# Linear attention: the pieces of FP4 unpacking moved away from the first q G products, and the sums for these products put in another order

## The chip, the cores and the metric

The kernel runs on one core of a Trainium2 chip. The core has five engines with an instruction queue each: TensorE (PE in the profile, its loading of weights PEld), VectorE (DVE), ScalarE (ACT), GpSimd (POOL) and SyncE (SP, here only an issuer of DMAs). Each engine takes its own instructions in their order, and waits on semaphores for the others. The metric is the device time of one execution in microseconds; the median of several runs counts.

## The reference, cut to what matters

Four blocks follow each other: a linear attention with a layer norm, an FP4 feed-forward part, a gated linear attention, and a routed feed-forward part. The change lies in the first one, on an input of 2 batches with 1024 rows of 512 values in float32:

```
q = elu(x Wq^T) + 1;   k = elu(x Wk^T) + 1;   v = x Wv^T        # 16 heads of 32
kv = k^T v  (per head);   z = 1 / (q . sum of k + 1e-6)
out = q kv z;   x = layernorm(x + out Wo^T)
```

The feed-forward part that comes next has weights in FP4, eight values in an int32, with a float16 scale per 128 inputs. Their unpacking (codes to float32) belongs to that part, but is done while the attention runs.

## The kernel before

**Blocks and batches.** The 2048 rows are 4 blocks of 512, two per batch; `b` counts batches, `i = 2b` and `j = 2b + 1` are a batch's blocks. The main loop is at L629 to L669: for each batch the k products of its blocks, then the q products, and in between the pieces of other work.

**Products by seven.** A 512x512 by 512x512 product is done with seven half-size products in place of eight (`by_seven`, L338). It needs sums of quarters: `sums_of_weights` (L330; T1, T2, T4, T3 from the weight's quarters B11 to B22, each one DVE instruction at L335) and three sums of x (S1 at L356, S2 at L357, S3 at L358, and again S2 at L373). The products accumulate into a bank of PSUM, `grow`: after each of them the partial sum is copied out by ACT (c11 at L363, c21 at L370, c22 at L376) or read by elu at L304 and L306, before PE adds the next product to the same bank. A second bank (`P` in the profile) takes the two products that are not part of the chain; DVE adds it at L366, L377 and L384. `elu1` (L299) is ACT, ACT, DVE: L304, L305, L306.

**k^T x and G.** `add_xk` (L393) accumulates k^T x of a batch in four banks; DVE and ACT copy it into G (L408). `values` (L452) multiplies by Wv (`vk`, copied by ACT at L463), `G_rows` (L465) by Wo (`gp`, 32 small matmuls at L473, copied into G by ACT at L477). G is now the batch's kv and Wo in one 512x512 matrix, so that out Wo^T is q G. `G_rows` then computes the four sums of G in the room `TG`: in batch 0 the tile staged[2], in batch 1 the slot in which Wo stood. The room's fourth quarter serves for S1 of q.

**q.** `weigh` (L436) divides each row of q by its sum with k: per 128 rows L441, L443, L444, L445 and L447, all on DVE. `turned` (L486) transposes 128 rows of q on PE (`qTp`, L217) and ACT copies them into qT (L492). `o_products` (L494) is q G by seven for a block: S1 (L515), S2 (L516), the difference A11 - A21 (L517), then seven products (L507), each followed by an add to x on DVE (L513). As elsewhere PE adds to `grow` only when the add to x has read it. It is a generator: `some_o(blk, n)` runs it n products on. For block 3 the product q G is a plain one, `whole_o` (L547).

**The 27 pieces of unpacking.** `unpack` (L244) is: a DMA issued by SP that brings 16 rows of packed words, each repeated on 8 partitions, into the tile `pk` (L248); two DVE instructions on it (L251, a pair of shifts, and L252, a mask); and a copy by ACT from float16 to float32r with a factor (L254). The pool has two `pk` buffers. The first 16 pieces are of 704 columns (352 KB, into wgu), the last 11 of 512 (256 KB, into wdn). `job(n)` (L616) puts n pieces at a point of the main loop.

**What sets the order.** A scheduler with a cost model of its own chooses each engine's order of instructions from the program's order and from what depends on what. `behind()` keeps PE's order to the program's, and `issue_after(anchor)` keeps a piece behind the last elu that was written before it. On the chip each engine then follows that order strictly: an instruction that waits for a DMA stops everything behind it on its engine.

**The steps of the loop.** `run(products, *others)` runs a generator of products and after each `yield` the next list of other steps. In batch 0 the q products of block 1 carry `turns(0, ...)`, `G_rows` and the q G products of block 0; in batch 1 the k products of block 2 carry the q G products of block 1; the q products of block 3 carry `G_rows` and the q G products of block 2, and `split_some`, which prepares the next part's input (L231, L232). Just behind the loop stand the scales of the next part: one small transpose `pg` (L679), a copy, and five small DVE instructions (L280, L281, L683, L684, L685); the first users are L807 (ACT) and L809 (DVE).

Of the kernel before, what the change touches and what calls it, by code (L numbers as in the profile page):

```python
# [10 lines left out]
F32 = mybir.dt.float32  # L11
# [10 lines left out]
P = 128  # L22
# [51 lines left out]
def body(ctx: ExitStack, tc: tile.TileContext, a: dict, out: bass.AP):  # L74
    nc = tc.nc
# [20 lines left out]
    def acc_bank(name):  # L96
        return bank("acc", name)
# [5 lines left out]
    staged = [  # L103
        wfp4.tile([P, to - at, C], F32, tag=f"wdn{i}", name=f"staged{i}")
        for i, (at, to) in enumerate(zip(wdn_parts, wdn_parts[1:]))
    ]
# [20 lines left out]
    def place_w(i, name):  # L127
        return wpool.tile([P, KC, C], F32, tag=f"A{i}", name=name)
# [27 lines left out]
    t, src = new_xT(0)  # L156
# [84 lines left out]
    wk = s1.enter_context(tc.tile_pool(name="s1", bufs=2))  # L241
# [85 lines left out]

    pieces_of = lambda t: t.rearrange("p (k c) -> p k c", k=2)

    def sums_of_weights(w, rooms):  # L330

        B11, B12, B21, B22 = (w[:, 2 * e : 2 * e + 2, 256 * o : 256 * o + 256] for e in range(2) for o in range(2))
        T1, T2, T4, T3 = (*rooms, B12)[:4]
        for dst, x, y in ((T1, B12, B11), (T2, B22, T1), (T4, B21, T2), (T3, B22, B12)):
            nc.vector.tensor_sub(dst, x, y)  # L335
        return T1, T2, T3, T4

    def by_seven(x, w, T, rooms, pairs, ready):  # L338
# [3 lines left out]
        T1, T2, T3, T4 = T  # L342
        S1, S2, S3 = rooms

# [11 lines left out]
        nc.vector.tensor_add(S1, A21, A22)  # L356
        nc.vector.tensor_sub(S2, S1, A11)  # L357
        nc.vector.tensor_sub(S3, A11, A21)  # L358
# [9 lines left out]
        yield  # L368
        product(grow, S2, T2, False)
        nc.scalar.copy(c21, p)  # L370
        side = mm_bank("P7")
        p7 = product(side, S3, T3, True)
        nc.vector.tensor_sub(S2, A12, S2)  # L373
        yield
# [4 lines left out]
        yield  # L379
        product(grow, S2, B22, False)  # L380
        elu1(c12, p)
# [8 lines left out]
    pairs_of, mv_of, G_of, acc_of, ksum_of = {}, {}, {}, {}, {}  # L390
# [59 lines left out]
    vkm_of, qT, TG, o_of, parts = {}, {}, {}, {}, []  # L450

    def values(b):  # L452
# [9 lines left out]

        nc.scalar.copy(vkm_of[b], vk.rearrange("p (c d) -> p c d", c=KC))  # L463

    def G_rows(b):  # L465


        gp = [acc_bank("gp") for _ in range(4)]
        quad = lambda i: slice(32 * i, 32 * i + 32)
        for j in range(4):  # L470
            for c in range(KC):
                with behind():
                    last_pe[0] = nc.tensor.matmul(  # L473
                        gp[j][quad(c)], vkm_of[b][quad(j), c, quad(j)], Wo[quad(j), c], start=True, stop=True
                    ).ins
        for c in range(KC):
            nc.scalar.copy(G_of[b][:, c], gp[c])  # L477

        room = staged[2] if b == 0 else place_w(3, "TG")
        rooms = slices(room, 0, 3)  # L480
        if b:

            rooms.append(pieces_of(wk.tile([P, 512], F32, tag="qT3", name="T3", bufs=1)))
        TG[b] = sums_of_weights(G_of[b], rooms), pieces_of(room[:, 3])

    def turned(blk, i):  # L486
        if i == 0:
# [6 lines left out]
    def o_products(blk):  # L494

        A11, A12, A21, A22 = (qT[blk][:, 2 * e : 2 * e + 2, 256 * t : 256 * t + 256] for t in range(2) for e in range(2))
        G = G_of[blk // 2]
        B11, _, B21, B22 = (G[:, 2 * e : 2 * e + 2, 256 * o : 256 * o + 256] for e in range(2) for o in range(2))
        (T1, T2, T3, T4), S1 = TG[blk // 2]
        S2 = pieces_of(wk.tile([P, 512], F32, tag="qS", name="qS", bufs=1))  # L500

        def product(ps, a, b, first, t, o):

            with behind():
                for r in range(2):
                    for k in range(2):
                        ins = nc.tensor.matmul(  # L507
                            ps[:, 256 * r : 256 * r + 256], a[:, k, r * P : (r + 1) * P], b[:, k],
                            start=first and r == 0 and k == 0, stop=k == 1, skip_group_check=True,
                        ).ins  # L510
            last_pe[0] = ins
            x = x_t[blk][:, 2 * t : 2 * t + 2, 256 * o : 256 * o + 256]
            nc.vector.tensor_add(x, x, ps.rearrange("p (r c) -> p r c", r=2))  # L513

        nc.vector.tensor_add(S1, A21, A22)  # L515
        nc.vector.tensor_sub(S2, S1, A11)  # L516
        nc.vector.tensor_sub(A21, A11, A21)  # L517
        grow = acc_bank("grow")
        product(grow, A11, B11, True, 0, 0)
        yield  # L520
        product(acc_bank("P2"), A12, B21, True, 0, 0)
        yield
        product(grow, S2, T2, False, 1, 0)
        nc.vector.tensor_sub(A12, A12, S2)
        yield
        side = acc_bank("P7")
        product(side, A21, T3, True, 1, 1)
        yield
        product(grow, S1, T1, False, 1, 1)
        yield  # L530
        product(side, A22, T4, False, 1, 0)
        yield
        product(grow, A12, B22, False, 0, 1)
        yield
        mv = mv_of[blk] = sp.tile([P, 4, 2], F32, tag="mv", name="mv")
        with tc.issue_after(weighed[0]):
            for i in range(4):
                row_stats(mv[:, i], x_t[blk][:, i])
            layernorm(x_t[blk], mv, by=nc.gpsimd)
        yield  # L540
# [57 lines left out]
    def some_xk(blk, *part):  # L598
        return [lambda i=i: add_xk(blk, i) for i in part]

    def turns(blk, *part):
        return [lambda i=i: turned(blk, i) for i in part]

    def some_o(blk, n):

        def one():
            if blk not in o_of:
                o_of[blk] = o_products(blk)
            next(o_of[blk])

        return [one] * n
# [4 lines left out]
    job = lambda n: [lambda: unpack_some(n)]  # L616
# [7 lines left out]
    step = lambda f, *x: [lambda: f(*x)]  # L624
# [4 lines left out]
    for b in range(B):  # L629
        i, j = 2 * b, 2 * b + 1  # L630
        if b:
            run(
                k_products(i),
                turns(1, 0, 1) + job(1), job(1),
                turns(1, 2, 3) + some_o(1, 1) + job(1), some_o(1, 2) + job(1), some_o(1, 5) + job(1),
            )
        q_ready = [] if b else step(q_weights)
        run(
            k_products(j), [],
            some_xk(i, 0, 1) + job(2), some_xk(i, 2) + job(1) + q_ready, some_xk(i, 3) + job(1), job(1 + b),  # L640
        )
        if b == 0:
            Ts["q"] = sums_of_weights(Wq, slices(staged[0], 0, 3))
        else:

            Tq = place_w(1, "Tq")
            for n in range(3):
                nc.scalar.copy(Tq[:, n], staged[0][:, n])
            Ts["q"] = (*slices(Tq, 0, 2), Ts["q"][2], *slices(Tq, 2, 3))
            S_rooms[0] = pieces_of(Tq[:, 3])  # L650
        run(
            q_products(i, lambda t: weigh(i, t)), [],
            some_xk(j, 0, 1) + job(1 + b), some_xk(j, 2) + step(spread_ksum, b) + job(1), some_xk(j, 3) + job(1 + b),
        )
        if b == 0:
            xT[2] = load_xT(2)
        split = [step(split_some, n) if b else [] for n in range(4)]
        rings["free"] = (rings["sum"][(turn_of["sum"] + 1) % 2],)
        run(
            q_products(j, lambda t: None),  # L660
            step(values, b),
            turns(i, 0, 1) + split[0] + job(1 - b),
            turns(i, 2, 3) + split[1] + step(G_rows, b),
            some_o(i, 2) + split[2] + some_o(i, 1) + job(1 - b),
            step(all_free) + some_o(i, 1) + step(weigh, j, 0) + split[3] + some_o(i, 3) + step(weigh, j, 1) + some_o(i, 1)
            + job(1 - b),
        )
        if b == 0:
            xT[3] = load_xT(3)  # L669
# [94 lines left out]
    with tc.tile_pool(name="s2", bufs=1) as wk2:  # L764
# [24 lines left out]
        class Chunk:  # L789
# [28 lines left out]
            def step(self, e, k, by):  # L818
                self.product(e, k)
                self.end(e, k, by)  # L820

        class Normed:
# [41 lines left out]
            def rest(self):  # L864

                for i in range(4):
                    x = x_t[self.blk][:, i]
                    nc.vector.scalar_tensor_tensor(x, self.y[:, i], self.ms[:, i : i + 1], x, ALU.mult, ALU.add)
                yield
                for i in range(4):  # L870
                    row_stats(self.mv[:, i], x_t[self.blk][:, i])
                layernorm(x_t[self.blk], self.mv)
# [179 lines left out]
    wk = s3.enter_context(tc.tile_pool(name="s3", bufs=1))  # L1052
# [368 lines left out]
    turns, last_hp = [0], [None]  # L1421
# [335 lines left out]
    wk = ctx.enter_context(tc.tile_pool(name="s4", bufs=2))  # L1757
# [4 lines left out]
    room = xT_tile("row")  # L1762
# [78 lines left out]
```

## Time and profile before

| | us |
|---|---|
| median of 3 runs | 934.13 |
| the 3 runs | 934.13, 934.41, 929.76 |
| the profiled execution | 929.62 |
| its span, first to last instruction | 927.8 |
| PE busy in the span | 900.6 (97%) |
| DVE busy | 685.2 (74%) |
| ACT busy | 377.3 (41%) |
| POOL busy | 257.4 (28%) |
| mean granted TensorE clock | 0.998 |

The prediction shows lines of four views. The page gives busy times and shares of the chain that ended last. A table by stretches has the length first, then the busy time of PE, PEld, DVE, ACT and POOL with the number of instructions, the granted clock, the DMA share and GB/s. A timeline has the start, the duration, the engine, the line of the code and the operation with its output and input tile; the bracket gives the idle time before it and what ended it. For a tile the profile lists its instructions and the time from a DMA's issue to its landing. Times in the text are from the span's start. The part of the program that the change touches runs from about 45 to 230 us.

### The profile page before, as it was taken

How to read it: one execution, taken by the hardware profiler on the slowest of the kernel's cores; microseconds unless marked ns; L12 is line 12 of the kernel's file. 1: busy time of each engine (PE TensorE's matmuls, PEld its weight loads, DVE VectorE, ACT ScalarE, POOL GpSimd, SP SyncE). 2: the span in 40 equal slices, each digit the busy share in tenths (PEclk: the TensorE clock that was granted, in tenths of full speed). 3: DMA queues.
4: the chain of work that ended last, by engine and by line, in shares of the span. 5: the costliest groups of instructions: out<-in, count | busy, mean ns of one | idle time of the engine just before them, and what ended most of it. 6: DMA issues, size and time to landing. Idle time of an engine off the chain costs nothing.

```text
span 927.8 us, 10966 instructions
## 1 busy us (share of the span) xinstructions
PE 900.6 (97%) x4037; PEld 698.6 (75%) x4037; DVE 685.2 (74%) x1310; ACT 377.3 (41%) x632; POOL 257.4 (28%) x229
## 2 busy tenths in 40 slices
PE   9999999999999999999998899999999999999996
PEld 6668876687677877877785577788676888888886
DVE  2579994689677786786686876676978886898635
ACT  2345334353476876876873524130311222120000
POOL 1020075100563555564563111010061030000012
PEclk9999999999999999999999999999999999999999
DMA  8622221100300001001001400000023211230011
GB/s 321 220 82 77 77 70 46 58 1 1 125 1 1 1 0 42 5 1 45 1 1 46 192 12 1 1 1 1 1 92 136 91 47 46 91 136 1 9 39 46
DMA packets 26136, 50.17 MB, mean 54 GB/s; under 512 B 4799, under 2 KB 5483, under 8 KB 25570
## 3 DMA queue, kind: packets, MB, share of 16 engines
q1 hardware_dynamic: 23441, 44.34, 14.0%
q0 software_dynamic: 1920, 4.22, 1.2%
q10 hardware_dynamic: 720, 0.92, 0.3%
q8 instruction: 32, 0.52, 0.2%
q14 instruction: 23, 0.18, 0.1%
HBM read 41.03 MB, written 10.54 MB: 56 GB/s over the span
## 4 chain that ended last, share of the span: by engine, by line
PE 76%; DVE 15%; ACT 3%; POOL 3%; issue 2%; DMA 1%; POOLq 0%; SPq 0%; ACTq 0%; DVEq 0%
PE yp L1525 10%; PE hp L1441 9%; PE gatep L783 8%; PE yp L783 8%; PE upp L783 8%; PE go L1196 6%; PE xk L400 6%; PE grow L349 4%; PE P L349 3%; PE ao L547 1%; PE ao L1314 1%; POOL x L884 1%; PE grow L1280 1%; PE kp L573 1%; DVE cmp L1365 1%
## 5 line engine op out<-in xcount | busy, mean ns | idle before, releaser
L841 DVE TENSOR_TENSOR yp<-yp,ratio 128x512 f32<-128x512 f32 x160 | 103.4, 694 | 13.1 <-PE yp L783 12.6
L201 POOL TENSOR_TENSOR rs<-rs,table 128x4 f32<-128x4 f32 (+1 forms) x20 | 18.2, 911 | 302.0 <-DVE rs L200 301.8
L807 ACT ACTIVATE gatep<-gatep,scale 128x512 f32<-128x512 f32 x132 | 85.3, 658 | 23.2 <-PE gatep L783 19.6
L783 PE MATMUL gatep<-x1Th,wgu 128*128 128x512 f32 x176 | 73.6, 418 | 0.6 <-ACT gatep L807 0.4
L783 PE MATMUL yp<-wdn,hlo 128*128 128x512 f32 x176 | 70.2, 399 | 3.4 <-POOL hlo L816 3.4
L783 PE MATMUL yp<-wdn,hhi 128*128 128x512 f32 x176 | 69.9, 397 | 2.0 <-POOL hhi L815 1.3
L783 PE MATMUL upp<-x1Th,wgu 128*128 128x512 f32 x176 | 69.3, 393 | 1.3 <-DVE whole L813 1.3
L783 PE MATMUL gatep<-x1Tl,wgu 128*128 128x512 f32 x176 | 69.3, 394 | 0.3 <-DVE x1Tl L232 0.3
L783 PE MATMUL upp<-x1Tl,wgu 128*128 128x512 f32 x176 | 68.9, 391 | 0.0
L813 DVE SCALAR_TENSOR_TENSOR whole<-upp,scale,silu 128x512 f32<-128x512 f32 x44 | 33.0, 751 | 38.1 <-PE upp L783 20.6
L807 ACT ACTIVATE upp<-upp,scale 128x512 f32<-128x512 f32 x82 | 54.3, 662 | 12.0 <-PE upp L783 8.2
L816 POOL TENSOR_TENSOR hlo<-whole,hhi 128x512 fp32r<-128x512 f32 x44 | 56.8, 1292 | 3.6
L815 POOL CAST hhi<-whole 128x512 fp32r<-128x512 f32 x44 | 26.9, 612 | 110.4 <-DVE whole L813 109.4
L809 DVE TENSOR_SCALAR upp<-upp,scale 128x512 f32<-128x512 f32 x50 | 37.5, 752 | 11.8 <-PE upp L783 11.1
L783 PEld LDWEIGHTS gatep<-x1Th,wgu 128*128 128x128 f32 x176 | 33.1, 188 | 15.1 <-DVE x1Tl L232 5.3
L1196 PE MATMUL go<-big 128*128 128x256 f32 x192 | 43.9, 381 | 0.0
L208 DVE BATCH_NORM_STATS2 st<-x 128x6 f32<-128x512 f32 x64 | 42.4, 678 | 0.4
L400 PE MATMUL xk<-pair,x 128*128 128x512 f32 x96 | 42.7, 592 | 0.0
L783 PEld LDWEIGHTS yp<-wdn,hlo 128*128 128x128 f32 x176 | 33.0, 188 | 12.3 <-POOL hlo L816 4.7
L783 PEld LDWEIGHTS yp<-wdn,hhi 128*128 128x128 f32 x176 | 33.0, 188 | 11.3 <-POOL hhi L815 2.8
L811 ACT ACTIVATE silu<-gatep,scale 128x512 f32<-128x512 f32 x44 | 30.2, 687 | 25.7 <-PE gatep L783 22.2
L1196 PEld LDWEIGHTS go<-big 128*128 128x128 f32 x192 | 35.9, 190 | 6.3 <-DVE q L1103 0.8
(450 smaller groups left out, 2092.5 us busy)
## 6 DMA issues: line engine op xcount, KB each, us to landing
pk<-in_gu SPq DMA_DIRECT2D x16, 352.0 KB, 3.7
x<-in_x SPq DMA_DIRECT2D x4, 1024.0 KB, 14.9
w<-in_w SPq DMA_DIRECT2D x1, 4096.0 KB, 12.2
xs<-picked SPq DMA_DIRECT2D x4, 1024.0 KB, 5.2
out<-x SPq DMA_DIRECT2D x4, 1024.0 KB, 4.2
w<-in_w SPq DMA_DIRECT2D x4, 1024.0 KB, 6.4
x0T<-in_xT SPq DMA_DIRECT2D x3, 1024.0 KB, 7.4
pk<-in_dn SPq DMA_DIRECT2D x11, 256.0 KB, 3.3
```

Source lines behind the costliest of these rows:

```text
L208: nc.vector.bn_stats(st, x)
L349: ins = nc.tensor.matmul(ps[:, 256 * r : 256 * r + 256], a[:, k, r * P : (r + 1) * P], b[:, k], start=first and r == 0 and k == 0, stop=k ...
L400: ins = nc.tensor.matmul(acc_of[b][c], x_t[blk][:, i, c * P : (c + 1) * P], pairs_of["k", blk][i // 2][:, i % 2], start=blk % 2 == 0 and i ...
L783: nc.tensor.matmul(ps, w, x, start=start and n == 0, stop=stop and n == 1, skip_group_check=True)
L807: nc.scalar.activation(ps, ps, AF.Copy, scale=s)
L809: nc.vector.tensor_scalar(ps, ps, s, None, ALU.mult)
L813: nc.vector.scalar_tensor_tensor(whole, ps, s, silu, ALU.mult, ALU.mult)
L816: nc.gpsimd.tensor_sub(lo, whole, hi.bitcast(F32))
L841: nc.vector.tensor_tensor(self.y[:, i] if g == NI - 1 else ps, ps, ratio[:, g], ALU.mult)
L1196: ins = nc.tensor.matmul(ps[:, 256 * m : 256 * m + 256], w[:, k, m], b[:, k, 256 * half : 256 * half + 256], start=first and m == 0 and k ...
L1441: ins = nc.tensor.matmul(ps[:, 256 * j : 256 * j + 256], w[:, k, 2 * g + j], x[:, k], start=k == 0, stop=k == 1).ins
L1525: nc.tensor.matmul(ps[:, 256 * r : 256 * r + 256], x(r, j), w(j), start=j == 0, stop=j == NJ - 1)
```

## The change

Three things are done.

1. The pieces of unpacking are moved. The numbers of pieces in the six runs of products before: 5 (k products of block 1), 3 (q products of block 0), 3 (q products of block 1), 5 (k products of block 2), 6 (k products of block 3), 5 (q products of block 2). After: 5, 5, 0, 1, 8, 8.
2. S1 and S2 of the batch's first q block are written by a function of their own, `q_sums`, called before `G_rows`. The room TG is taken at that point.
3. `G_rows` writes T1 and T2 only; T4 and T3 are written in `o_products` behind the first product's add to x, and A11 - A21 behind them.

```diff
-    def sums_of_weights(w, rooms):
+    def sums_of_weights(w, rooms, part=range(4)):
...
-        for dst, x, y in ((T1, B12, B11), (T2, B22, T1), (T4, B21, T2), (T3, B22, B12)):
-            nc.vector.tensor_sub(dst, x, y)
+        steps = (T1, B12, B11), (T2, B22, T1), (T4, B21, T2), (T3, B22, B12)
+        for i in part:
+            nc.vector.tensor_sub(*steps[i])
...
+    def TG_room(b):
+        if b not in TG_rooms:
+            TG_rooms[b] = staged[2] if b == 0 else place_w(3, "TG")
+        return TG_rooms[b]
+
+    TG_rooms, TG_rest, S_of = {}, [], {}
+
+    def q_sums(blk):
+
+        A11, A12, A21, A22 = (qT[blk][:, 2 * e : 2 * e + 2, 256 * t : 256 * t + 256] for t in range(2) for e in range(2))
+        S1 = pieces_of(TG_room(blk // 2)[:, 3])
+        S2 = pieces_of(wk.tile([P, 512], F32, tag="qS", name="qS", bufs=1))
+        nc.vector.tensor_add(S1, A21, A22)
+        nc.vector.tensor_sub(S2, S1, A11)
+        S_of[blk] = S1, S2
...
-        TG[b] = sums_of_weights(G_of[b], rooms), pieces_of(room[:, 3])
+        TG[b] = sums_of_weights(G_of[b], rooms, range(2))
+        TG_rest.append(lambda: sums_of_weights(G_of[b], rooms, range(2, 4)))
...
-        nc.vector.tensor_add(S1, A21, A22)
-        nc.vector.tensor_sub(S2, S1, A11)
-        nc.vector.tensor_sub(A21, A11, A21)
+        if blk not in S_of:
+            q_sums(blk)
+        S1, S2 = S_of[blk]
         grow = acc_bank("grow")
         product(grow, A11, B11, True, 0, 0)
+        for rest in TG_rest:
+            rest()
+        TG_rest.clear()
+        nc.vector.tensor_sub(A21, A11, A21)
...
                 k_products(i),
-                turns(1, 0, 1) + job(1), job(1),
-                turns(1, 2, 3) + some_o(1, 1) + job(1), some_o(1, 2) + job(1), some_o(1, 5) + job(1),
+                turns(1, 0, 1), [],
+                turns(1, 2, 3) + some_o(1, 1), some_o(1, 2), some_o(1, 5) + job(1),
...
             k_products(j), [],
-            some_xk(i, 0, 1) + job(2), some_xk(i, 2) + job(1) + q_ready, some_xk(i, 3) + job(1), job(1 + b),
+            some_xk(i, 0, 1) + job(2), some_xk(i, 2) + job(1 + b) + q_ready, some_xk(i, 3) + job(1 + b), job(1 + b),
...
             q_products(i, lambda t: weigh(i, t)), [],
-            some_xk(j, 0, 1) + job(1 + b), some_xk(j, 2) + step(spread_ksum, b) + job(1), some_xk(j, 3) + job(1 + b),
+            some_xk(j, 0, 1) + job(2 + b), some_xk(j, 2) + step(spread_ksum, b) + job(1 + b), some_xk(j, 3) + job(2 + b),
...
             q_products(j, lambda t: None),
             step(values, b),
-            turns(i, 0, 1) + split[0] + job(1 - b),
-            turns(i, 2, 3) + split[1] + step(G_rows, b),
-            some_o(i, 2) + split[2] + some_o(i, 1) + job(1 - b),
-            step(all_free) + some_o(i, 1) + step(weigh, j, 0) + split[3] + some_o(i, 3) + step(weigh, j, 1) + some_o(i, 1)
-            + job(1 - b),
+            turns(i, 0, 1) + split[0],
+            turns(i, 2, 3) + split[1] + step(q_sums, i) + step(G_rows, b),
+            some_o(i, 2) + split[2] + some_o(i, 1),
+            step(all_free) + some_o(i, 1) + step(weigh, j, 0) + split[3] + some_o(i, 3) + step(weigh, j, 1) + some_o(i, 1),
```

More of the change, by code (lines that the diff above doesn't have):

```diff
@@ L477, in G_rows @@
             nc.scalar.copy(G_of[b][:, c], gp[c])
-        room = staged[2] if b == 0 else place_w(3, "TG")
+        room = TG_room(b)
         rooms = slices(room, 0, 3)
@@ L498, in o_products @@
         B11, _, B21, B22 = (G[:, 2 * e : 2 * e + 2, 256 * o : 256 * o + 256] for e in range(2) for o in range(2))
-        (T1, T2, T3, T4), S1 = TG[blk // 2]
-        S2 = pieces_of(wk.tile([P, 512], F32, tag="qS", name="qS", bufs=1))
+        T1, T2, T3, T4 = TG[blk // 2]
         def product(ps, a, b, first, t, o):
```

## The prediction

> **What bounds the kernel now.** I read the page first, then the busy time by stretches, the timeline of TensorE (PE) with what ended its idle time, the timeline of all engines where the moved pieces land, and the instructions on the tile `pk`.
>
> The page: engines' busy shares, and the chain that ended last.
> ```profile
> PE 900.6 (97%) x4037; PEld 698.6 (75%) x4037; DVE 685.2 (74%) x1310; ACT 377.3 (41%) x632; POOL 257.4 (28%) x229
> ...
> PE 76%; DVE 15%; ACT 3%; POOL 3%; issue 2%; DMA 1%; POOLq 0%; SPq 0%; ACTq 0%; DVEq 0%
> ```
> PE is the bound. A change off PE helps only where PE waits, and hurts where it makes PE wait.
>
> Busy time by stretch (length, then PE, PEld, DVE, ACT, POOL):
> ```profile
> 72.00:92.00 20.00, 19.75 (x138) 16.33 (x136) 19.23 (x39) 10.65 (x20) 0.00 (x0) 1.00 0.28 89
> 92.00:105.00 13.00, 11.71 (x52) 9.69 (x53) 11.94 (x24) 3.82 (x6) 0.00 (x0) 1.00 0.33 108
> 160.00:187.00 27.00, 27.00 (x94) 17.37 (x92) 16.52 (x29) 12.23 (x22) 5.25 (x4) 1.00 0.15 49
> ```
> Around the first q G products DVE is full and PE idles; in the q products of batch 1 (last row) PE never idles and DVE has 10 us spare. All idle time of PE over 0.25 us between 60 and 210 us, with what ended it:
> ```profile
> 92.47 1.99 PE L507 MATMUL grow<-staged,qS 128*128 128x256 f32 x8 [0.72 <-DVE x L513]
> 104.19 1.99 PE L507 MATMUL grow<-G,staged 128*128 128x256 f32 x8 [0.68 <-DVE x L513]
> 120.57 1.99 PE L507 MATMUL grow<-staged,qS 128*128 128x256 f32 x8 [0.55 <-DVE qS L516]
> 131.59 1.99 PE L507 MATMUL grow<-G,staged 128*128 128x256 f32 x8 [0.39 <-DVE x L513]
> 207.41 1.99 PE L507 MATMUL grow<-TG,qS 128*128 128x256 f32 x8 [0.98 <-DVE x L513]
> ```
> That is all there is to win: 3.3 us, 0.36%. Products that wait for nothing start 1.73 us apart (88.14, 89.86), so the first gap costs 92.47-89.86-1.73 = 0.88, the third (from 118.13) 0.71, the fourth (from 129.31) 0.55.
>
> Where pieces and PE meet, in three places (start, duration, engine, line):
> ```profile
> 59.71 0.58 DVE L251 TENSOR_SCALAR pk<-pk,shift 128x704 int32<-128x704 int32 x1 [1.95 <-DMA pk<-in_gu]
> 61.59 0.57 ACT L370 COPY pair<-grow 128x512 f32<-128x512 f32 x1
> 63.58 1.89 PE L349 MATMUL grow<-staged,Tk 128*128 128x256 f32 x8
> ...
> 175.64 0.49 DVE L251 TENSOR_SCALAR pk<-pk,shift 128x512 int32<-128x512 int32 x1 [2.96 <-DMA pk<-in_dn]
> ...
> 179.23 0.59 ACT L376 COPY pair<-grow 128x512 f32<-128x512 f32 x1 [1.03 <-PE grow L349]
> ...
> 182.47 1.89 PE L349 MATMUL grow<-Wq,rw 128*128 128x256 f32 x8
> ...
> 190.41 1.28 DVE L447 TENSOR_TENSOR pair<-pair,z 128x512 f32<-128x512 f32 x2
> ...
> 192.95 1.04 PE L217 MATMUL qTp<-table,pair 128*128 128x128 f32 x8
> ```
> A piece that DVE reaches before its data have landed stops DVE, and its ACT half (L254) then stops ACT. The copies L370 and L376 empty `grow` before PE adds the next product to it; the transposes (L217) need L447. How long a landing takes:
> ```profile
> DMA to landing us min/median/max: 3.2/3.5/4.0
> ```
> Two `pk` buffers: a load starts when ACT ends the piece two before. At 55.88 a load was issued and DVE began at 59.71, 3.84 us later; the small pieces of wdn took 3.42 (143.18 to 146.60) and 3.43 (172.21 to 175.64). One buffer's cycle was 175.64-170.57 = 5.07 us.
>
> **The change, part by part.** In the order of instructions after the change, PE's is the same but for one small transpose (`pg`), and POOL's is the same. The 27 pieces went 5, 3, 3, 5, 6, 5 to the six runs of products; now 5, 5, 0, 1, 8, 8. Times below are on the clock of the kernel before; each wait shifts what follows.
>
> *Piece 8, batch 0.* It now stands on DVE behind piece 7, and on ACT ahead of L370. Its buffer came free at 58.58 and the load was issued at 58.61; landed at 58.61+3.84 = 62.45. L251 to L252 0.62, to ACT's L254 0.56, to L370 0.70, L370 0.57: grow is empty at 64.90, and PE, ready at 63.58, starts at 64.95: **+1.4** (with landings of 3.2 and 4.07 us, as rows have them, 0.8 and 1.6). DVE's L373 goes from 60.77 to 63.6, covered: PE needs it at 68.74.
>
> *Pieces 9 and 10* stand ahead of L357 on DVE and of L305 on ACT (L304 70.67, two L254 at 0.69, L305 ends 73.30 instead of 72.41), so the weighing starts 0.3 later, with no idle DVE after it until the weighed row that ends at 83.79 and whose transposes start at 83.88: **+0.26**. On SP one more load stands ahead of the x0T load issued at 72.39; it lands in 7.4 and is used at 106.02, covered. One fewer stands ahead of the next x0T load.
>
> *First G products of block 0.* Two pieces are gone. The scheduler kept all four sums of G ahead of the first add to x here. But without L254 at 85.97 ACT's four copies of G run from 85.2 instead of 86.66, bounded by the last matmul into gp (ends 86.38), and end at 87.3 instead of 88.69. DVE: S1 85.3, then at 0.6 each S2, A21, four sums, L377, L356, the add to x at 90.7, ending 91.38; PE is ready at 91.59. **-0.83** of 0.88. The gaps at 101.51 and 104.19 follow a chain that begins with PE at 96.2 (L304, L305, L306, L384, ...) and stay: 0.
>
> *Block 1.* Three pieces (six instructions of 0.49 to 0.59 us) leave 108 to 120. S1 can start when ACT has copied the last transposes (115.9), S2 ends about 117.3, the add to x at 118; PE is ready at 119.86. **-0.71**. But piece 11 stands between L306 (1.75 us beside POOL's sum) and the add to x that PE waits for at 131.59. L306 can start 0.8 earlier, L251 took 1.27 beside POOL: the add ends some 0.5 later. **+0.5** (-0.55 if POOL is out of the way, +1.3 if not and L306 gains nothing).
>
> *k products of block 3, eight pieces:* DVE had 14.12 busy us of 25 there (135 to 160). The closest case is L306 of the pair, 161.1 instead of 160.1 for matmuls at 162.48: covered, 0.
>
> *q products of block 2, eight pieces instead of five.* By the 5.07 cycle, pieces 20, 22, 24 come to DVE at 170.57, 175.64, 180.70. Piece 24 stands ahead of L356, L377 and the copies of G on DVE, and on ACT ahead of L426 and L376. L254 181.68, L426 182.24, L376 182.75 to 183.35: PE's product of 182.47 starts at 183.40, **+0.93**. Then L377 183.4, both copies of G, L306 (two ACT steps after L377) 185.8; pieces 25 and 26 186.4 to 188.05; L357; L384 ends 189.33. `vk` takes the bank that L384 empties and would have started at 188.4: **+1.0**. Piece 27 now stands ahead of the weighing: its load is issued when ACT ends piece 25 (188.33), lands at 191.75, and holds DVE, idle from 190.8. From there the weighing goes on at its own pitch (piece 27 and L306 inside it): the second weighed row ends at 198.05 instead of 191.69, the fourth at 203.3 instead of 198.16. PE, 1.95 late by then, is held to 198.1 where it was at 193.28 (4.8 late), and to 203.35 where it was at 198.21: **+3.2**. Sum here +5.1; 0 if all lands early, +6 if POOL's sum (1.75 for 0.68) stretches pieces 18 and 19 again.
>
> *Block 2's G products.* S1 and S2 stand ahead of their old places, T3 behind the add to x. S1's room is Wo's, so S1 waits for gp's matmuls (200.6) with T1 behind it, which waits for ACT's copy (201.44) anyhow. T1 201.5, S2, T2 (last copy 202.42), L377, T4, add to x 204.5 instead of 206.67; PE is ready at 206.43. **-0.98**. `pg` (0.24) falls into the wait before the last transposes. Two L809 now precede L447 at 224.41: 1 us late at most, transposes at 226.47, 0 to +0.1.
>
> **Sum:** +1.4+0.26-0.83-0.71+0.5+5.1-0.98 = **+4.7**; on the profiled 929.62 us 934.3. The profiled execution is 4.51 under the runs' median (934.13), 0.14 under their fastest (929.76): the runs stand at two levels. The same addition on the median gives 938.8. I say 936, between the two.
>
> *A rule that speaks against the rows.* The Trainium skill, "SBUF — State Buffer", section "The DMA setup-cost knee", has a transfer take some 2 us plus its bytes over 436 GB/s: 2.8 us for 352 KB, 2.6 for 256 KB. By that estimate the first wait shrinks to 0.4, the chain of batch 1 to about 1.0, and the sum is -0.4. The measured 3.84 and 3.43 decide.
>
> **The rivals.**
> *Half the price:* landings near the shortest row (3.2, or under). Piece 24 no longer holds L376, piece 27 still delays the weighing by some 2 us: +1.6, 931.2. Against it: the 3.42 to 3.46 of four waits.
> *Faster:* no moved piece is waited for, only the gaps go: -0.83-0.71-0.98 = -2.5, 927.1. For it: DVE has 10 idle us in the last row shown. It decides if piece 8 lands by 61.1, 2.5 us after its issue; no landing was under 3.2.
> *It does not do what it says:* T3 and T4 stay ahead of block 0's first add to x; if the copies of G come no earlier either, that gap stays and the sum is +5.5, 935.1.
>
> **How the numbers follow.** Forecast 0.60, half price 0.17, faster 0.13, undone 0.10. Range: from the faster case between the levels (928) to the sum with its upper ends on the median (+7.4, 941.5). Half a per cent, about what a measurement can tell here, is 4.65 us, just under the sum: of the forecast and the undone case (0.70) two thirds lie beyond it, 0.48, and a little of half price 0.02. Of the faster case only a run at the lower level shows beyond -0.5%: 0.09 with the levels' scatter. The rest, 0.41, is no change.
>
> **What would show it.** Right: PE's gaps at 92, 120 and 207 gone; new idle time of PE before grow L349 near 64 (released by ACT) and near 187, before vk, and before qTp near 200 (by DVE), with DVE idle on `pk` loads just before. Wrong: DVE never idle on those loads, or ACT's copies of grow ahead of the pieces; or the pieces beside POOL's work stretch to twice their time in 140 to 155, a wait that I priced at nothing.

## The result, and the profile after

| | us | of the time before |
|---|---|---|
| before, median of 18 runs (929.76 to 934.41) | 931.94 | |
| after, median of 18 runs (931.99 to 937.7) | 934.28 | 1.0027, 95% interval 1.0016 to 1.0038 |
| span of the profiled execution, before and after | 927.8 and 931.7 | |

The change costs 2.3 us by the medians, 2.5 by the ratio. The 95% interval lies above 1, so it is slower; the loss stays inside the half per cent that the prediction called no change. The prediction said 936.0, in 928 to 941.5.

The page of the kernel after: busy times, and the shares of the chain that ended last.
```profile
PE 901.1 (97%) x4037; PEld 698.2 (75%) x4037; DVE 685.0 (74%) x1310; ACT 377.0 (40%) x632; POOL 256.7 (28%) x229
...
PE 68%; DVE 11%; issue 10%; POOL 6%; ACT 3%; DMA 2%; SPq 0%; POOLq 0%; DVEq 0%; ACTq 0%
```
Every engine does the same work as before, to within 1 us. PE is busy 0.5 us longer in a span 3.9 us longer: the difference is idle time of PE. (From the chain's shares little is read: PE's is 68 to 81% in the kernels shown below too.) The timeline of PE between 40 and 240 us, the part that the change touches, lists the waits there (start, duration, instruction, and in the bracket the idle time with what ended it).
```profile
65.77 1.99 PE L350 MATMUL grow<-staged,Tk 128*128 128x256 f32 x8 [1.11 <-ACT pair L371]
105.96 1.99 PE L524 MATMUL grow<-G,staged 128*128 128x256 f32 x8 [0.68 <-DVE x L530]
184.12 1.99 PE L350 MATMUL grow<-Wq,rw 128*128 128x256 f32 x8 [1.20 <-ACT pair L377]
189.96 3.84 PE L460 MATMUL vk<-G,Wv 128*128 128x128 f32 x32 [0.40 <-DVE pair L385]
196.93 0.66 PE L217 MATMUL qTp<-table,pair 128*128 128x128 f32 x4 [1.40 <-DVE pair L448]
198.23 0.66 PE L217 MATMUL qTp<-table,pair 128*128 128x128 f32 x4 [0.65 <-DVE pair L448]
203.45 0.66 PE L217 MATMUL qTp<-table,pair 128*128 128x128 f32 x4 [0.16 <-DVE pair L448]
223.10 0.50 PE L803 MATMUL gatep<-x1Tl,wgu 128*128 128x512 f32 x1 [0.42 <-DVE x1Tl L232]
```
Line numbers have moved: L349 is now L350, L370 L371, L376 L377, L384 L385, L447 L448, L507 L524, L513 L530. Of the five gaps of before, those at 92, 121, 132 and 207 us are gone and the one near 104 has stayed. Six new ones stand ahead of products that need what ACT or DVE hands over; the last row was there before, with 0.30.

Both kernels issue the same products in the same order but for the one small transpose `pg`. So each product of after can be set beside its twin of before, and the difference of their starts is how late PE is. The steps of that difference, in us:

| place (start before) | step | what PE waits for there, now or before |
|---|---|---|
| 7.57, first load of all | +0.91 | the input's data; no changed instruction has run yet |
| 63.58, grow of block 0 | +1.27 | ACT's copy L371 |
| 83.99, transposes of q | +0.30 | DVE's L448 |
| 92.47, q G of block 0 | -0.71 | gone: the add to x |
| 120.57, q G of block 1 | -0.72 | gone: S2 |
| 131.59, q G of block 1 | -0.66 | gone: the add to x |
| 182.47, grow of block 2 | +1.25 | ACT's copy L377 |
| 187.65, vk | +0.67 | DVE's L385 |
| 192.95, 193.38, 198.22, transposes of q | +1.66, +0.87, +0.39 | DVE's L448 |
| 207.41, q G of block 2 | -1.15 | gone: the add to x |
| the rest, to the end | -0.25 | steps of 0.1 to 0.3 of both signs |

Losses 6.41 us, gains 3.24 and 0.25: +2.9 us in the two profiled executions, once the first 0.91 is left out; +2.3 between the medians.

Why PE waits at 65.77 and in batch 1 is seen in the timeline of all engines. Batch 0:
```profile
63.27 0.59 DVE L251 TENSOR_SCALAR pk<-pk,shift 128x704 int32<-128x704 int32 x1 [1.94 <-DMA pk<-in_gu]
...
64.45 0.79 ACT L254 ACTIVATE wgu<-pk 128x704 fp32r<-128x704 f16 x1 [2.29 <-DVE pk L252]
65.15 0.57 ACT L371 COPY pair<-grow 128x512 f32<-128x512 f32 x1
```
The load was issued by SP at 59.27:
```profile
59.27 0.54 SPq L248 DMA_DIRECT2D pk<-in_gu  x1
```
So DVE got piece 8 4.00 us after the issue, at 63.27; ACT is held 2.29 us ahead of the piece's copy, and the copy of grow stands behind it in ACT's queue. The same in batch 1:
```profile
181.50 0.49 DVE L251 TENSOR_SCALAR pk<-pk,shift 128x512 int32<-128x512 int32 x1 [2.07 <-DMA pk<-in_dn]
...
182.48 0.63 ACT L254 ACTIVATE wdn<-pk 128x512 fp32r<-128x512 f16 x1 [2.98 <-DVE pk L252]
...
183.48 0.59 ACT L377 COPY pair<-grow 128x512 f32<-128x512 f32 x1
...
190.73 0.69 DVE L306 SCALAR_TENSOR_TENSOR pair<-grow,e 128x512 f32<-128x512 f32 x1 [0.83 <-ACT e L305]
192.13 0.49 DVE L251 TENSOR_SCALAR pk<-pk,shift 128x512 int32<-128x512 int32 x1 [0.70 <-DMA pk<-in_dn]
...
195.58 0.69 DVE L306 SCALAR_TENSOR_TENSOR pair<-pair,e 128x512 f32<-128x512 f32 x1
196.19 0.68 DVE L448 TENSOR_TENSOR pair<-pair,z 128x512 f32<-128x512 f32 x1
...
196.95 0.63 DVE L442 TENSOR_TENSOR qk<-pair,ksum 128x512 f32<-128x512 f32 x1
```
Piece 24 holds ACT until 182.48 and so L377 to 183.48; piece 27 holds DVE in the weighing, and its first weighed row (L448) comes at 196.19, after which PE starts at 196.93. Not all of this loss is waiting for a load. From the end of the first L306 shown (191.43) to the end of the second weighed row (198.18) DVE takes 2.46 us more than in before (187.40 to 191.69): 0.70 is idle time for piece 27's load, 0.74 the piece's own two instructions, and 1.16 the second L306 and an L442, which the scheduler now orders ahead of the second row (0.14 is saved elsewhere).

### The profile page after: what moved, and what is told of

Same layout as the page of the kernel before. It is cut to its first block, busy times and chain, and to the rows that moved or that the text cites. A ratio compares the mean times of both kernels' runs of the same rounds, so it can differ in the third digit from the quotient of the medians.

```text
span 931.7 us, 10974 instructions
## 1 busy us (share of the span) xinstructions
PE 901.1 (97%) x4037; PEld 698.2 (75%) x4037; DVE 685.0 (74%) x1310; ACT 377.0 (40%) x632; POOL 256.7 (28%) x229
## 4 chain that ended last, share of the span: by engine, by line
PE 68%; DVE 11%; issue 10%; POOL 6%; ACT 3%; DMA 2%; SPq 0%; POOLq 0%; DVEq 0%; ACTq 0%
PE yp L1545 10%; PE hp L1461 9%; PE yp L803 8%; PE gatep L803 7%; PE upp L803 7%; PE go L1216 6%; PE grow L350 3%; PE xk L401 3%; POOL x L904 2%; PE P L350 2%; PE ao L1334 1%; PE grow L524 1%; PE grow L1300 1%; PE kp L594 1%; DVE cmp L1385 1%
```

## The experiments

Theory A: the loss is the wait for pieces that DVE reaches before their data have landed, carried to PE by what stands behind them in DVE's and ACT's queues; the sums of q and G only help. Rival B: the loss comes from the sums' new order. Rival C: it is the work of the extra pieces in their new runs, wherever their data are. Each kernel ran beside the kernel before, whose median was 930.51 us in the first four and 930.52 us in the last four.

### The sums alone

The kernel before with the sums of the kernel after, and every piece where it was.

```diff
-        TG[b] = sums_of_weights(G_of[b], rooms), pieces_of(room[:, 3])
+        TG[b] = sums_of_weights(G_of[b], rooms, range(2))
+        TG_rest.append(lambda: sums_of_weights(G_of[b], rooms, range(2, 4)))
...
+        for rest in TG_rest:
+            rest()
...
-            turns(i, 2, 3) + split[1] + step(G_rows, b),
+            turns(i, 2, 3) + split[1] + step(q_sums, i) + step(G_rows, b),
```

> Only the sums' part of the change: S1 and S2 of the batch's first q block ahead of G's copies, T4 and T3 behind the first add to x; all pieces of unpacking stand as before the change. The scheduler then orders batch 0 as before and changes block 2's sums alone. Theory A (the loss is pieces that are waited for, the sums only help): TensorE's wait of 0.98 us before the third product of block 2 goes, nothing else moves: -1.0 us, ratio 0.999. Rival B (the loss comes from the sums, S1 waiting for Wo's room at the head of VectorE's queue): at least +2 us, ratio 1.002 or more.

Measured: 929.36 us, 0.9983 (0.9971 to 0.9995). PE's timeline:
```profile
93.16 2.00 PE L524 MATMUL grow<-staged,qS 128*128 128x256 f32 x8 [0.72 <-DVE x L530]
...
121.25 2.00 PE L524 MATMUL grow<-staged,qS 128*128 128x256 f32 x8 [0.55 <-DVE qS L479]
132.71 2.00 PE L524 MATMUL grow<-G,staged 128*128 128x256 f32 x8 [0.83 <-DVE x L530]
```
The gap at 207 is gone (-1.15 against before), the three of batch 0 are still there. The scheduler's order of DVE differs from before in block 2 only. The gap near 132 is longer all the same, 0.83 where the profiled execution of before has 0.39, and PE 0.43 later behind it: POOL's copy ahead of its sum ends 0.43 later there. So the size of this gap is not fixed by the order of instructions; what the sums win is -1.15, and the whole trace shows -0.9. Rival B falls: the sums' new order is a gain, and its place is the second batch.

### The pieces alone

The changed numbers of pieces (5, 5, 0, 1, 8, 8) with `sums_of_weights`, `G_rows` and `o_products` as before:

```diff
-            some_xk(j, 0, 1) + job(1 + b), some_xk(j, 2) + step(spread_ksum, b) + job(1), some_xk(j, 3) + job(1 + b),
+            some_xk(j, 0, 1) + job(2 + b), some_xk(j, 2) + step(spread_ksum, b) + job(1 + b), some_xk(j, 3) + job(2 + b),
...
-            turns(i, 0, 1) + split[0] + job(1 - b),
+            turns(i, 0, 1) + split[0],
```

> Only the pieces are moved (5, 5, 0, 1, 8, 8); all sums as before the change. Theory A: all waits of the changed kernel for landings are there (TensorE held by about 1.3 near 64, 0.3 near 86, 4.8 between 182 and 204), the gaps of blocks 0 and 1 are gone (-0.7 each, and -0.7 at the last product of block 1), only block 2's gain of 1.0 is missing: +4.1 us, ratio 1.0044. Rival B: no loss without the sums' move: -2 us or 0.

Measured: 935.42 us, 1.0052 (1.0033 to 1.0070). All six new waits are there with nearly the same sizes (1.04 for 1.20 differs most), the gap at 207 is back, and those at 92, 121 and 132 are gone by the same 0.70, 0.72 and 0.66:
```profile
65.59 2.00 PE L349 MATMUL grow<-staged,Tk 128*128 128x256 f32 x8 [1.05 <-ACT pair L370]
...
183.81 1.99 PE L349 MATMUL grow<-Wq,rw 128*128 128x256 f32 x8 [1.04 <-ACT pair L376]
...
196.63 0.66 PE L217 MATMUL qTp<-table,pair 128*128 128x128 f32 x4 [1.41 <-DVE pair L447]
...
212.35 2.00 PE L507 MATMUL grow<-TG,qS 128*128 128x256 f32 x8 [0.98 <-DVE x L513]
```
So the moved pieces make all of the loss and all of batch 0's gain; the sums make the -1.15. The two kernels' ratios add to 1.0035, against 1.0027 for the whole change.

### A third buffer for the pieces

The changed kernel with three `pk` buffers, so that a load starts one piece earlier. The room comes from three small tiles that share others' places.

```diff
-    dq = s1.enter_context(tc.tile_pool(name="dq", bufs=2))
+    dq = s1.enter_context(tc.tile_pool(name="dq", bufs=3))
...
-        raw = wk.tile([n, 2, P], F16, name="dn_raw", bufs=1)
+        raw = wk.tile([n, 2, P], F16, tag="gu_scale", name="dn_raw", bufs=1)
...
-        s = wk.tile([n, 2, P], F32, name="dn_scale", bufs=1)
+        s = wk.tile([n, 2, P], F32, tag="qT3", name="dn_scale", bufs=1)
...
-    spare_scale = wk.tile([P, KC * FG], F32, name="gu_scale", bufs=1)
+    spare_scale = wk.tile([P, KC * FG], F32, tag="gu_scale", name="gu_scale", bufs=1)
```

> The changed kernel with three buffers for the packed words in place of two (the room comes from letting four small tiles of the scales share slots); same pieces at the same points of the program. Theory A: a load is then issued one piece earlier, at least 2.5 us, and no piece is waited for where TensorE stands behind it: the waits of 1.3, 0.3 and 4.8 us go, the gains of 3.4 stay: -3.4 us against the kernel before the change, ratio 0.9964. Rival C (the eight instructions more on VectorE and ScalarE in these stages cost by their busy time, not by the landing): as the changed kernel, +2.5 us, ratio 1.0027.

Measured: 927.54 us, 0.9965 (0.9953 to 0.9977). All idle time of PE between 40 and 240 us that the timeline lists:
```profile
104.12 2.00 PE L524 MATMUL grow<-G,staged 128*128 128x256 f32 x8 [0.68 <-DVE x L530]
196.97 0.65 PE L217 MATMUL qTp<-table,pair 128*128 128x128 f32 x4 [0.21 <-DVE pair L448]
216.63 0.50 PE L803 MATMUL gatep<-x1Tl,wgu 128*128 128x512 f32 x1 [0.30 <-DVE x1Tl L232]
```
and around piece 8, which is still ahead of L371 on ACT:
```profile
57.88 0.59 DVE L251 TENSOR_SCALAR pk<-pk,shift 128x704 int32<-128x704 int32 x1 [0.54 <-DMA pk<-in_gu]
...
59.06 0.79 ACT L254 ACTIVATE wgu<-pk 128x704 fp32r<-128x704 f16 x1 [0.65 <-DVE pk L252]
59.76 0.57 ACT L371 COPY pair<-grow 128x512 f32<-128x512 f32 x1
```
The place in ACT's queue is the same, the copy of grow comes at 59.76 instead of 65.15 (0.5 of that is the start), and PE waits for nothing there. The pieces' work is the same too, so rival C falls as the account of the whole: what costs is that the data come late. One reservation: with three buffers the scheduler also set some other pieces and the weighing's steps in another order, so the run doesn't show that each single wait went for this reason alone. That holds for the weighing above all, whose steps are back in the order of before: the 2.92 us lost at its transposes go with the wait, the piece's work there and the order together.

The control, the kernel before with the same third buffer:

> The kernel before the change with the same third buffer: the control for the one above. Theory A: in the kernel before, VectorE waits for landings (11 us in all) but TensorE stands behind none of them, so nothing is to be won: 0 within 0.7 us, ratio 0.999 to 1.001. If the third buffer helps by itself (a rival to A's reading of the run above): -1 us or more, ratio under 0.999.

Measured: 930.61 us, 1.0001 (0.9989 to 1.0013). The kernel before had no wait of PE behind a piece, and a third buffer gives it nothing.

### Piece 8 in another place, two buffers

```diff
-                turns(1, 0, 1), [],
+                turns(1, 0, 1), job(1),
...
-            some_xk(j, 0, 1) + job(2 + b), some_xk(j, 2) + step(spread_ksum, b) + job(1 + b), some_xk(j, 3) + job(2 + b),
+            some_xk(j, 0, 1) + job(2 + b), some_xk(j, 2) + step(spread_ksum, b) + job(2 * b), some_xk(j, 3) + job(2 + b),
```

> The changed kernel with one piece less in the q products of block 0 (piece 8, in the middle of that run) and one more in the k products of block 2, behind the first two transposes of block 1. Theory A (waits for landings): PE's wait of 1.11 us before grow L350 near 65.8 us goes, and with it 1.27 us; in its new place the piece has landed long before DVE comes to it, and the add to x behind it ends about 0.6 us later, in time for PE at 121.6. Everything else as in the changed kernel. So 1.27 us less than the changed kernel's +2.5: 1.0013 of the time before. Rival C (the work of a moved piece costs, not its landing): the 1.27 us only move to the new place, 1.0027. A third possibility: the gap at 120.6 comes back, +0.7, 1.0021.

Measured: 933.12 us, 1.0022 (1.0010 to 1.0033). Here DVE's and ACT's order differ from the changed kernel's in this one piece only. PE's wait at 65.77 is gone, and against the changed kernel PE is 1.27 us earlier from there on, to the hundredth what was expected; at the new place nothing is lost. The median shows less of it than the trace: 1.0013 was expected. It meets the number of the third case (1.0021), but not what that case says: the timeline has no gap near 120. In the profiled execution PE lost 1.6 us again near 492 us, far behind the change, where the granted clock was lower; only one of this kernel's 11 runs had a mean clock of 0.998, and it took 931.35 us, 1.0 over the kernel before at that clock (the last section), where the trace has 1.5 by 480 us.

### Three pieces of batch 1 behind the loop, two buffers

```diff
-            some_xk(j, 0, 1) + job(2 + b), some_xk(j, 2) + step(spread_ksum, b) + job(1 + b), some_xk(j, 3) + job(2 + b),
+            some_xk(j, 0, 1) + job(2), some_xk(j, 2) + step(spread_ksum, b) + job(1), some_xk(j, 3) + job(2),
```

> The changed kernel with five pieces in place of eight in the q products of block 2; the three that are left are unpacked behind the loop, where the scheduler puts them among the last weighing (about 205 to 225 us). Two buffers. Theory A: the waits at 184.1, 190.0, 196.9, 198.2 and 203.5 us go (1.25+0.67+1.66+0.87+0.39 = 4.84 us), the gains at 92, 121, 132 and 207 us stay (3.24 us), the loss in batch 0 stays (1.57 us): -1.7 us, 0.9982. If the last three pieces hold DVE at the last weighing, up to 2 us come back: 1.0003. Rival C: DVE and ACT do the same work in all, so little changes against the changed kernel: 1.0027.

Measured: 928.79 us, 0.9978 (0.9967 to 0.9990). PE's starts, against the changed kernel, step by -1.35, -0.67, -1.66, -0.87 and -0.39 at the five places: 4.94 us, where the losses there were 4.84. As with the third buffer, the weighing's steps are back in the order of before. The last three pieces stand in the last weighing, and no wait of PE shows there:
```profile
65.36 1.99 PE L350 MATMUL grow<-staged,Tk 128*128 128x256 f32 x8 [0.90 <-ACT pair L371]
105.56 1.99 PE L524 MATMUL grow<-G,staged 128*128 128x256 f32 x8 [0.68 <-DVE x L530]
217.77 0.50 PE L803 MATMUL gatep<-x1Tl,wgu 128*128 128x512 f32 x1 [0.30 <-DVE x1Tl L232]
```

### Both moves, two buffers

```diff
-                turns(1, 0, 1), [],
+                turns(1, 0, 1), job(1),
...
-            some_xk(j, 0, 1) + job(2 + b), some_xk(j, 2) + step(spread_ksum, b) + job(1 + b), some_xk(j, 3) + job(2 + b),
+            some_xk(j, 0, 1) + job(2), some_xk(j, 2) + step(spread_ksum, b) + job(b), some_xk(j, 3) + job(2),
```

> The two moves together (piece 8 in the k products of block 2, three pieces behind the loop), two buffers. Theory A: the savings add: -1.7 - 1.27 = -2.9 us, 0.9968, the same as the changed kernel with three buffers (0.9965); only the 0.30 us of pieces 9 and 10 is left of the losses. Rival C: 1.0027. If the last three pieces hold the last weighing: up to 0.999.

Measured: 927.72 us, 0.9956 (0.9939 to 0.9972). The savings add, without a third buffer: near 480 us PE is 3.2 us ahead of before, the difference of the start taken off. This kernel and the changed one with three buffers are both faster than the kernel before and the kernel after; they can't be told apart.

### Two pieces where the prediction's step failed

```diff
-                turns(1, 2, 3) + some_o(1, 1), some_o(1, 2), some_o(1, 5) + job(1),
+                turns(1, 2, 3) + some_o(1, 1), some_o(1, 2), some_o(1, 5) + job(2),
...
-            some_xk(i, 0, 1) + job(2), some_xk(i, 2) + job(1 + b) + q_ready, some_xk(i, 3) + job(1 + b), job(1 + b),
+            some_xk(i, 0, 1) + job(2 - b), some_xk(i, 2) + job(1 + b) + q_ready, some_xk(i, 3) + job(1 + b), job(1 + b),
```

> The changed kernel with two pieces in place of one at the end of the k products of block 2, ahead of the add to x that PE waits for near 132 us, and one piece less in the next run. It tests the step of the prediction that failed: the piece there was given 1.27 us and a loss of 0.5 us; it took 0.57 us and PE lost nothing there, because it fell between two of POOL's sums. If a piece beside POOL's sum is as slow as the prediction had it, the second one falls beside POOL's next sum (130.6 to 133.6 us), takes about 1.27 us, the add to x ends near 132.9 and PE's product starts about 0.95 us later than in the changed kernel. If DVE isn't slowed there at all, the second takes 0.57 us and PE loses 0.15 us. The rest as in the changed kernel: +3.4 us and 1.0037 of the time before in the first case, 1.0029 in the second.

Measured: 935.67 us, 1.0046 (1.0029 to 1.0062). The timeline of all engines:
```profile
129.11 2.08 DVE L251 TENSOR_SCALAR pk<-pk,shift 128x704 int32<-128x704 int32 x2
129.33 2.98 POOL L420 TENSOR_TENSOR ksum<-ksum,pair 128x512 f32<-128x512 f32 x2 [0.69 <-DVE pair L306]
131.12 0.67 DVE L530 TENSOR_TENSOR x<-x,grow 128x512 f32<-128x512 f32 x1
...
131.84 1.99 PE L524 MATMUL grow<-G,staged 128*128 128x256 f32 x8 [0.97 <-DVE x L530]
```
The two L251 took 2.08 us together: the first 0.57, as in the changed kernel, the second 1.58 beside POOL's sum (the trace has them overlap a little). PE's product starts 1.08 us later than in the changed kernel, the first of the two cases expected.

## Why the prediction was right or wrong

**Right: the mechanism and the size of nearly every term.** In us, predicted and measured:

| step of the prediction | predicted | measured |
|---|---|---|
| Piece 8, batch 0 | +1.4 | +1.27 |
| Pieces 9 and 10 | +0.26 | +0.30 |
| First G products of block 0 | -0.83 | -0.71 |
| Block 1, the gap at 120.57 | -0.71 | -0.72 |
| Block 1, the gap at 131.59 | +0.5 | -0.66 |
| k products of block 3 | 0 | 0 |
| q products of block 2: L376, vk, the weighing | +0.93, +1.0, +3.2 | +1.25, +0.67, +2.92 |
| Block 2's G products | -0.98 | -1.15 |

The experiments bear out the reasons behind the terms, and not their sum alone. Piece 8's wait was priced with a landing of 3.84 us; it took 4.00 (59.27 to 63.27) and its loss goes with the piece. The gains of batch 0 come from the pieces alone, that of batch 1 from the sums alone, as the steps had it.

**Wrong: "Block 1", the piece between L306 and the add to x, +0.5 where -0.66 came.** It makes 1.16 of the 1.8 us between the predicted sum of 4.7 and the measured 2.9. The step took L306 at 1.75 us and the piece's L251 at 1.27, as the kernel before had them. The timeline of before there:
```profile
128.58 0.68 DVE L357 TENSOR_TENSOR rw<-Tk,x0T 128x512 f32<-128x512 f32 x1
128.62 1.77 POOL L419 TENSOR_TENSOR ksum<-ksum,pair 128x512 f32<-128x512 f32 x1
...
129.19 1.75 DVE L306 SCALAR_TENSOR_TENSOR pair<-pair,e 128x512 f32<-128x512 f32 x1
...
130.86 0.68 DVE L513 TENSOR_TENSOR x<-x,grow 128x512 f32<-128x512 f32 x1
```
and of after:
```profile
128.65 1.27 POOL L420 TENSOR_TENSOR ksum<-ksum,pair 128x512 f32<-128x512 f32 x1
128.74 0.69 DVE L530 TENSOR_TENSOR x<-x,P 128x512 f32<-128x512 f32 x1 [0.88 <-PE P L524]
129.34 1.13 DVE L306 SCALAR_TENSOR_TENSOR pair<-pair,e 128x512 f32<-128x512 f32 x1
...
130.40 0.57 DVE L251 TENSOR_SCALAR pk<-pk,shift 128x704 int32<-128x704 int32 x1
130.62 3.01 POOL L420 TENSOR_TENSOR ksum<-ksum,pair 128x512 f32<-128x512 f32 x2 [0.69 <-DVE pair L306]
130.90 0.67 DVE L530 TENSOR_TENSOR x<-x,grow 128x512 f32<-128x512 f32 x1
131.99 1.89 PE L524 MATMUL grow<-G,staged 128*128 128x256 f32 x8
```
In before POOL's sum begins with DVE's L357 and takes 1.77 us, and L306 ends 0.55 us behind POOL (130.94 and 130.39). In after, with the pieces gone, the same DVE sum (L358 there) runs at 125.28; beside POOL's sum stands an add to x that reads P. POOL takes 1.27, ends at 129.92, and L306 again ends 0.55 behind it (130.47). L251 starts 0.22 us ahead of the second of POOL's sums and keeps its 0.57, though the two overlap, and the add is done 0.4 us before PE needs it. The step carried durations of before to a place where the neighbour that made them had left; the alternative that it named, -0.55 "if POOL is out of the way", is near what came. That a piece there does take 1.6 us when it falls beside the sum is shown by the run with two of them. That L357's place is what made POOL's sum longer is read from the traces, not tried: in the ten profiled kernels, POOL's sum took 1.77 us in the three with that DVE sum beside it, and 1.27 or 1.28 in the seven without. And the gap itself, 0.39 in the profiled execution of before, is 0.83 and 0.81 in the two other kernels with its order there (the sums alone; before with a third buffer), so the -0.66 is the gain over this one execution.

The Trainium skill, "SBUF — State Buffer", section "Who interferes with whom", says that a VectorE instruction with two inputs in SBUF contends with a GpSimd instruction that reads SBUF, that one with at most one such input, outside the two-port modes, doesn't, and that the pair of ports that they share is an exclusive lock. L306's end 0.55 us behind POOL's in both kernels agrees with a lock, and the unhindered add that reads P from PSUM (0.69 us) with the second.

**Mis-sized.** Of batch 1's three terms one was 0.3 too small and two 0.3 too large. PE came to the product at 182.47 half a us earlier than on the clock of before (1.57 lost, 2.09 won by then), which the step did not subtract, and so waited longer for L377. Piece 27 came to DVE at 192.13, less 0.91 for the start 191.22, where the step had 191.75; so the weighing was held less. The sum is near: 5.13 predicted, 4.84 measured.

**The level.** The prediction took the three runs of before (929.76, 934.13, 934.41) for two levels and put its forecast between the sums on them, 934.3 and 938.8. The lower one is what the median after came to (934.28), by two errors of opposite sign: the profiled execution is 2.3 under the median of 18 runs before (931.94), and the sum is 2.4 over the medians' difference. That the median fell on it is luck. The 18 runs lie between 929.76 and 934.41 with their median in the middle: two levels were read into three runs (what the scatter goes with, the last section tells). The +7.4 at the upper end of its range isn't worked out there; the upper ends that its steps name add to +6.7.

**The rivals.** By the number alone the measured +2.9, or +2.3 by the medians, is nearer to "half the price" (+1.6) than to the forecast's +4.7; the rows decide between them. "Half the price" had the landings near 3.2 us; piece 8's took 4.0, and piece 24 did hold L376. "Faster" (-2.5) needed no wait for any moved piece; its gains came as it had them, and with the waits removed by a buffer or by moving four pieces it is what one gets: -3.0 and -2.8 us in the medians. The 3.3 us that the prediction called all there is to win was the idle time of five gaps; the four that went had 2.64 of it and gave 3.24 by PE's starts, so idle time understates what a gap costs here. "It does not do what it says" fell: the gap at 92 is gone although all four sums stay ahead of the add to x.

**The rule weighed against the rows.** The tile `pk` in the profile of after:
```profile
  DMA pk<-in_gu: 9.3, 4
  DMA pk<-in_dn: 6.7, 5
...
DMA to landing us min/median/max: 3.0/3.6/6.8
```
DVE sat idle 16.0 us for nine landings, where it was 11.1 us for six before. The estimate by the Trainium skill's "SBUF — State Buffer", section "The DMA setup-cost knee" (2.8 and 2.6 us for these sizes) lies under the shortest landing that the trace gives, 3.0. By it the change would have been a gain; the measurement decided.

## What to carry to other kernels

Ahead of moving work that waits for a load, look up when its buffer comes free and when the load lands, and what stands behind it in the queue of each engine that handles it: here a copy of 0.6 us behind a piece of 0.8 us passed 1.27 us of a wait of 1.94 on to the engine that bounds. Idle time of an engine is no room for such work if its data come later than the room; a third buffer, or another place for four of 27 pieces, made +2.5 us into -3. And a duration that was stretched by a neighbour is to be carried over only with the neighbour: look first whether the change moves it.

## What was not expected of the hardware

**The runs' scatter goes with the granted clock.** Four of the profiled executions lost 1.6 to 3.9 us of PE between 489 and 547 us, in code that the change does not touch, and two more lost 0.7. By stretches (length, busy times, then the granted clock, the DMA share and GB/s), the kernel with both moves:
```profile
480.00:515.00 35.00, 30.00 (x130) 20.93 (x129) 25.02 (x38) 17.54 (x29) 12.38 (x12) 0.98 0.28 107
515.00:550.00 35.00, 32.40 (x139) 21.38 (x138) 26.94 (x45) 9.88 (x23) 6.61 (x7) 0.88 0.15 59
```
The profiled executions of before and after have 1.00 in both stretches. Every run has a mean granted clock, and the time goes with it: over 52 runs of the kernel before (those beside the experiments) the correlation is -0.92, with 0.7 us more for each 0.001 less. Their median is 930.3 us at 0.998 and 0.999 (30 runs), 932.1 at 0.997 (14) and 934.2 at 0.993 (5). This is probably what the prediction took for two levels; the clock of its three runs is not on record. At 0.998 or more alone, and so without most of the scatter, the differences to before are:

| kernel | runs | median, us | less 930.3 | PE's start near 480 us, later than in before |
|---|---|---|---|---|
| after (its 18 runs, beside other runs of before) | 7 | 933.0 | +2.7 | +3.0 |
| sums alone | 8 | 929.1 | -1.2 | -0.9 |
| pieces alone | 3 | 934.5 | +4.2 | +4.1 |
| after, third buffer | 6 | 926.9 | -3.4 | -3.0 |
| before, third buffer | 9 | 930.6 | +0.3 | +0.4 |
| piece 8 later | 1 | 931.4 | +1.0 | +1.5 |
| three behind the loop | 3 | 928.2 | -2.2 | -2.2 |
| both moves | 2 | 926.0 | -4.3 | -3.2 |
| two pieces at 131 | 1 | 934.7 | +4.4 | +4.3 |

The last column is read from the profiled execution of each kernel, ahead of the stretch with the lower clock, with the difference of the start taken off. The +0.4 of the control, and 0.4 in the row of the sums alone, is the longer gap near 132. The two columns agree to half a us except for both moves, where two runs stand against one trace. What sets the clock from one execution to the next stays open.

**The start.** The data of the first load of all came 0.91 us later in the profiled execution of after than in that of before, and 0.3 us earlier to 0.8 later in the others, ahead of any changed instruction. A difference of two spans is to be read from a ledger of matched instructions, not from the spans.

Left open: the 0.30 us of pieces 9 and 10, and the gap of 0.68 near 104 us that every kernel here has, were not tried.
